# Two rows broadcast by way of DRAM, filler products on TensorE, and a later place for the sums in the first group of a graph-attention kernel

## The chip, the core and the metric

The kernel runs on one core of a Trainium2 chip. The core has five engines that run beside each other and wait for each other through semaphores: TensorE (PE, with its weight loads shown apart as PEld), VectorE (DVE), ScalarE (ACT), GpSimd (POOL) and SyncE (SP). Transfers between DRAM and the on-chip memory are issued from SP's and ScalarE's instruction streams and carried out by 16 DMA engines. The metric is the device time of one execution in microseconds (us); lower is better.

## What is computed

Two graph layers follow each other, on 64 graphs of 256 nodes with 512 features (x: 64 x 256 x 512, adj: 64 x 256 x 256, all float32). The first is a single-head attention in which the score of a pair of nodes is a sum of two numbers, q of the one and k of the other:

```python
feat_proj = einsum('bnh,oh->bno', feats, fc_w) + fc_b
q = einsum('bnh,oh->bno', feat_proj, q_w) + q_b
k = einsum('bnh,oh->bno', feat_proj, k_w) + k_b
masked = q + swapaxes(k, 2, 1) + (1.0 - adj) * -1e9
masked = where(masked >= 0, masked, 0.01 * masked)
x1 = einsum('bnm,bmh->bnh', softmax(masked), feat_proj) + feats
```

The second is an attention with 8 heads over x1, with the logarithm of the adjacency and a bias added to the scores, and x1 added to its output.

Since q and k are one number per node, the kernel does not go through feat_proj for them: it multiplies q_w and k_w with fc_w once, which gives two rows of 512 numbers, and takes the dot product of each node's features with these rows. The rows, here called q's row (`wq_row`) and k's row (`wk_row`), are needed in all 128 partitions. How they get there is what the change is about.

## The kernel before

The 64 graphs are worked in 32 groups of two (512 nodes, as T = 4 tiles of 128). A function `step` writes out by hand the order of all engines' work for one group's tail, the next group's middle and the one after it; inside the block `tc.manual_schedule` each engine takes its instructions in exactly the order of the program. Groups 1 to 31 take their first layer in pieces mixed with the heads of the group before. Group 0 has nothing to be mixed with, and its first layer is the function `features_first` (L678), which runs in the first 45 us or so. The changed lines all lie there or ahead of it.

**Loads.** ScalarE issues the four pieces of fc_w, `fc_nat` (L225). SP issues q_w, k_w and fc_b (L231), x of group 0 (L206), b_q and b_v (L231), q_b and k_b (L138), the four pieces of adj of group 0 (L201), then the weights wq, wk and wv of 1 MB each (L143) and `wgc_row` (L138). The adj pieces of group 1 (L201) follow in `step`. An adj piece is 128 KB in runs of 128 bytes.

**Warm-up and rows.** TensorE first multiplies the identity with itself six times (L1143, result unused), turns the small vectors into columns (`columns`, L249), and then `rows_of_x` (L257) forms both rows at once: four products accumulate in one PSUM bank, the product with piece `oc` of `fc_nat` as soon as that piece has landed (L261). ScalarE copies the 2 x 512 result to the on-chip memory (L266). `constant` (L279) forms a small constant `kqc`; its end, `k_constant`, is called later.

**Spreading.** `spread_rows` (L269) is called after the first tile of x has been transposed (L691). For each row, a product with a column of the identity, repeated 128 times, puts the row into all partitions of a PSUM bank (L273), and ScalarE copies it out (L277).

**features_first**, in the order of its engines:

- TensorE transposes the four tiles of x (`xTp`, L686; VectorE copies them, L687) and fc_w (`pfc`, L152; ScalarE copies it to `fcT`, L153). `product(t)` forms feat_proj of tile t (`fp`, L699; ScalarE copies it, L703).
- VectorE takes the dot products with q's row (`dot_q`, four instructions L519, in the trace `jq`), then `k_constant` (L291), then those with k's row (`dot_k`, `jk`), then `adjt` (the transposed adjacency L557 and the mask L559).
- `queries` (L572): four TensorE transposes spread q of the nodes along the free axis (L576), and ScalarE copies the result to `qrow` (L581).
- `weights(jc)` (L593), for two halves: VectorE adds q, k and mask (L599) and applies the slope (L603), ScalarE takes the Exp (L604). The result `e0` holds the unnormalised attention. `add_eps` (L570) prepares the adjacency for the second layer.
- `constants_of_projections` (L295): products of fc_b with wq and wv (`pc`, L301). Its end, `add_constants` (L310), transposes the result (`pct`, L313) and adds it to the bias columns (VectorE, L317 and L318).
- `blocks_of_weights` (L327): sums of blocks of wk, wq and later wv and fcT on VectorE (L335 to L338).
- `sums` (L633): products of a column of ones with `e0` (L639) give the softmax sums, ScalarE copies them (L644). `recip_of_sums` (L646): one transpose (`rc`, L648), and VectorE's reciprocal (L649).
- For each tile t, the product of `e0` with feat_proj (`x1p`, L731), two of the block sums on VectorE, the scaling and the addition of x (VectorE, L737), and then the transpose of the new x (`x1Tp`, L792) with ScalarE's copies (L797).

After this, `step` begins the second layer of group 0 with the first product of Q (`pq`, L412).

**Later groups** spread q of the nodes in another way, `spread` (L583): SP writes the 512 numbers to DRAM (`q`, L586) and reads them back to all partitions (`qrow`, L588).

PSUM is used in four single banks (`bank`) and two pairs. The constant's bank (`pk`) is kept from `constant` until `k_constant`.

Of the kernel before, what the change touches and what calls it, by code (L numbers as in the profile page):

```python
# [10 lines left out]
F32 = mybir.dt.float32  # L11
# [6 lines left out]
P = 128  # L18
# [7 lines left out]
def kernel(  # L26
# [64 lines left out]
    nc = tc.nc  # L91
    NB, N, D = x.shape
# [4 lines left out]
    NC = D // P  # L97
# [12 lines left out]
    const = ctx.enter_context(tc.tile_pool(name="const", bufs=1))  # L110
# [5 lines left out]
            name=nc.get_next_instruction_name(), act_func_set_id=both[0], ins=[], outs=[]  # L116
# [4 lines left out]
    ident = const.tile([P, P], F32, tag="ident", name="ident")  # L121
# [24 lines left out]
    def transposed_weights(w, pool, psum, copy):  # L146

        t = pool.tile([P, NC, D], F32, tag="fcT", name="fcT")
        for hc in range(NC):
            pt = psum.tile([P, 512], F32, tag="bank", name=f"pfc_{hc}")  # L150
            for oc in range(NC):
                nc.tensor.transpose(pt[:, ts(oc, P)], w[:, oc, ts(hc, P)], ident)  # L152
            copy(t[:, hc, :], pt)  # L153
        return t

    wk_row = const.tile([P, D], F32, tag="wk_row", name="wk_row")
    wq_row = const.tile([P, D], F32, tag="wq_row", name="wq_row")
    kqc = const.tile([P, 1], F32, tag="kqc", name="kqc")

    NR = 4  # L160
# [3 lines left out]
    def fast():  # L164
        main = ExitStack()
        with main:
# [12 lines left out]
            def bank(name):  # L179
                return ps.tile([P, 512], F32, tag="bank", name=name)  # L180

            def pair(name):
                return psc.tile([P, 2, 512], F32, tag="pair", name=name)

            dram = main.enter_context(
                tc.tile_pool(name="dram", bufs=2, space=bass.MemoryType.DRAM)
            )
# [30 lines left out]
            for q in range(P // B):  # L218
                for n in range(P // B):
                    rows = slice(q * B, (q + 1) * B)  # L220
# [24 lines left out]
            def columns(rows, cols, name):  # L245

                n = rows.shape[0]
                pt = bank(name)
                nc.tensor.transpose(pt[:, 0:n], rows, ident[0:n, 0:n])  # L249
                nc.vector.tensor_copy(cols, pt[:, 0:n])  # L250
# [6 lines left out]
            def rows_of_x():  # L257

                pr = bank("rows_qk")[0:2, :]
                for oc in range(NC):  # L260
                    nc.tensor.matmul(  # L261
                        pr, lhsT=cols_0[:, oc : oc + NC + 1 : NC], rhs=fc_nat[:, oc, :],
                        start=(oc == 0), stop=(oc == NC - 1),
                    )
                rows = one.tile([2, D], F32, tag="junk", name="rows_qk_sb")
                nc.scalar.copy(rows, pr)  # L266
                return rows

            def spread_rows(rows):  # L269

                for n, dst in enumerate((wq_row, wk_row)):
                    pt = bank(f"row_{n}")
                    nc.tensor.matmul(  # L273
                        pt, lhsT=ident[0:2, n : n + 1].to_broadcast([2, P]), rhs=rows,
                        start=True, stop=True,
                    )
                    nc.scalar.copy(dst, pt)  # L277

            def constant():  # L279

                both = two.tile([P, NC], F32, tag="c", name="qk_col")
                part = two.tile([P, 2, T], F32, tag="kq", name="qk_fcb")
                nc.vector.tensor_tensor(both, qw_col, kw_col, ALU.add)
                nc.vector.tensor_tensor(both, both, fcb_col, ALU.mult)
                nc.vector.tensor_reduce(part[:, 0, 0:1], both, AX.X, ALU.add)
                pk = bank("pk")
                nc.tensor.matmul(
                    pk[:, 0:1], lhsT=part[:, 0, 0:1].to_broadcast([P, P]), rhs=ones[:, 0, 0:1],
                    start=True, stop=True,
                )  # L290
                return lambda: nc.vector.scalar_tensor_tensor(  # L291
                    kqc, pk[:, 0:1], qb, kb, ALU.add, ALU.add
                )
# [232 lines left out]
            class Group:  # L526
# [151 lines left out]
                def features_first(self):  # L678

                    g = self.g  # L680
                    xT = one.tile([P, NC, TOK], F32, tag="qT", name=f"xT_{g}")
                    fp = v_all
                    for t in range(T):
                        pt = bank(f"xTp_{g}_{t}")
                        for c in range(NC):
                            nc.tensor.transpose(pt[:, ts(c, P)], self.x[:, t, ts(c, P)], ident)  # L686
                        nc.vector.tensor_copy(  # L687
                            xT[:, :, ts(t, P)], pt.rearrange("p (c n) -> p c n", c=NC)
                        )
                        if t == 0:  # L690
                            spread_rows(rows_qk)  # L691
                    fcT = transposed_weights(fc_nat, wts, ps, nc.scalar.copy)
                    for t in range(T):
                        self.dot_q(t)

                    def product(t):
                        pp = bank(f"fp_{g}_{t}")
                        for c in range(NC):
                            nc.tensor.matmul(  # L699
                                pp, lhsT=xT[:, c, ts(t, P)], rhs=fcT[:, c, :],  # L700
                                start=(c == 0), stop=(c == NC - 1),
                            )
                        nc.scalar.copy(fp[:, t, :], pp)  # L703

                    product(0)
                    self.queries()
                    k_constant()
                    for t in range(T):
                        self.dot_k(t)
                    self.adjt(True)  # L710
                    product(1)
                    self.weights(0)
                    self.weights(1)
                    self.add_eps()
                    product(2)
                    add_constants = constants_of_projections()
                    for name, wt in (("k", wk_sb), ("q", wq_sb)):
                        for issue in blocks_of_weights(wt, name):
                            issue()
                    self.sums()  # L720
                    columns(rows_1, cols_1, "cols_1")
                    product(3)
                    add_constants()
                    self.recip_of_sums()
                    self.begin()
                    sums = blocks_of_weights(wv_sb, "v") + blocks_of_weights(fcT, "fc")
                    for t in range(T):
                        gr, ic = divmod(t, TPG)
                        po = bank(f"x1p_{g}_{t}")
                        for j in range(TPG):  # L730
                            nc.tensor.matmul(  # L731
                                po, lhsT=self.e0[:, j, gr, ts(ic, P)], rhs=fp[:, gr * TPG + j, :],
                                start=(j == 0), stop=(j == TPG - 1),
                            )
                        for issue in sums[2 * t : 2 * t + 2]:
                            issue()
                        nc.vector.scalar_tensor_tensor(  # L737
                            self.x[:, t, :], po, recip0[:, g, t : t + 1], self.x[:, t, :],
                            ALU.mult, ALU.add,
                        )  # L740
                        if t > 0:
                            self.x1t(t - 1)
                    self.x1t(T - 1)
# [393 lines left out]
            with tc.manual_schedule(engines=ENGINES):  # L1137
                f = Group(0)
                f.x, f.a = x_0, adj_0

                warm = bank("warm")
                for n in range(6):
                    nc.tensor.matmul(warm[:, 0:P], lhsT=ident, rhs=ident, start=True, stop=True)  # L1143
                columns(rows_0, cols_0, "cols_0")
                rows_qk = rows_of_x()
                k_constant = constant()
                d, a, a_w = None, None, {}
                for g in range(NG):
                    n = Group(g + 1) if g + 1 < NG else None

                    def check():

                        if d is not None and (d.g % NR == NR - 1 or d.g == NG - NR // 2 - 1):
                            in_range(d.g // NR * NR, d.g + 1, f"{d.g}")

                    step(d, a, f, n, check)
                    d, a, f = a, f, n
# [215 lines left out]
```

## Time and profile before

| What | us |
|---|---|
| runs of the kernel | 2314.91, 2314.97, 2316.4 |
| median of the runs | 2314.97 |
| the profiled execution, own time | 2316.6 |
| its span, first to last instruction | 2314.8 |
| busy in the span: TensorE, VectorE, ScalarE, GpSimd | 2298.1, 2111.0, 1073.2, 122.5 |
| first `pq` product of group 0 on the chain of waits | 45.23 |

The profiled execution is one execution; its span leaves out what lies before the first and after the last instruction, 1.8 us. Its mean granted TensorE clock is 0.997 of full speed.

A row of the timeline or of the chain begins with the start in us from the start of the span and the duration in us; then come the engine, the line, the operation, the tile written and the tiles read. In brackets stands how long the engine was idle before it and what ended that. "PE row L273 x4" are the four instructions of the two row products: a float32 product is two instructions. In a table by stretches of time, each engine's busy time is followed by the number of its instructions; PEclk is the clock that TensorE was granted, and the DMA share is the mean busy share of the 16 DMA engines (a little over 1 where packets overlap). "SPq" and "ACTq" are the instruction streams of SP and ScalarE from which transfers are issued. In the view of the waits a line says who waited for whom: us in total, times, longest.

### The profile page before, as it was taken

How to read it: one execution, taken by the hardware profiler on the slowest of the kernel's cores; microseconds unless marked ns; L12 is line 12 of the kernel's file. 1: busy time of each engine (PE TensorE's matmuls, PEld its weight loads, DVE VectorE, ACT ScalarE, POOL GpSimd, SP SyncE). 2: the span in 40 equal slices, each digit the busy share in tenths (PEclk: the TensorE clock that was granted, in tenths of full speed). 3: DMA queues.
4: the chain of work that ended last, by engine and by line, in shares of the span. 5: the costliest groups of instructions: out<-in, count | busy, mean ns of one | idle time of the engine just before them, and what ended most of it. 6: DMA issues, size and time to landing. Idle time of an engine off the chain costs nothing.

```text
span 2314.8 us, 33829 instructions
## 1 busy us (share of the span) xinstructions
PE 2298.1 (99%) x12738; PEld 1910.7 (83%) x12738; DVE 2111.0 (91%) x3150; ACT 1073.2 (46%) x1865; POOL 122.5 (5%) x120
## 2 busy tenths in 40 slices
PE   9999999999999999999999999999999999999997
PEld 5888888888888888888888888888888888888885
DVE  6899999999899999999999999999999999999997
ACT  3544445444445444444444454444544444444443
POOL 0000000000000000000000000000000000000000
PEclk9999999999999999999999999999999999999999
DMA  4122323323323232232233232332323323323312
GB/s 132 42 64 73 78 73 69 65 65 84 80 63 70 60 78 78 73 66 63 69 78 82 60 74 63 79 78 74 64 60 73 78 74 69 69 61 84 81 46 38
DMA packets 517265, 163.85 MB, mean 71 GB/s; under 512 B 415188, under 2 KB 478696, under 8 KB 517096
## 3 DMA queue, kind: packets, MB, share of 16 engines
q1 hardware_dynamic: 514440, 160.32, 29.4%
q8 instruction: 103, 1.69, 0.3%
q10 hardware_dynamic: 2656, 1.31, 0.2%
q14 instruction: 66, 0.54, 0.1%
HBM read 95.43 MB, written 66.12 MB: 70 GB/s over the span
## 4 chain that ended last, share of the span: by engine, by line
PE 97%; DVE 1%; DMA 1%; ACT 0%; issue 0%; SPq 0%; ACTq 0%; DVEq 0%
PE pv L412 17%; PE pq L412 16%; PE pf L412 16%; PE pk L412 16%; PE sc L840 11%; PE oT L880 10%; PE y L670 9%; PE fp L699 1%; DMA fc_nat<-in_L_gnn_fc_w_dram 0%; PE tot L907 0%; PE rc L624 0%; DMA xd<-xt 0%; PE xTp L686 0%; DVE osb L1003 0%; DVE osb L1009 0%; DVE osb L1002 0%
## 5 line engine op out<-in xcount | busy, mean ns | idle before, releaser
L854 ACT ACTIVATE e<-sc,c 128x1024 f32<-128x1024 f32 x254 | 269.0, 1110 | 81.7 <-PE sc L840 80.2
L860 DVE TENSOR_TENSOR e<-e,am 128x1024 f32<-128x1024 f32 x254 | 297.8, 1213 | 0.4 <-ACT e L854 0.4
L840 PE MATMUL sc<-qT,kT 64*128 64x256 f32 x2048 | 255.8, 389 | 0.3 <-ACT e L854 0.3
L880 PE MATMUL oT<-e,v 128*64 128x256 f32 x2032 | 233.4, 382 | 0.0
L495 POOL TENSOR_TENSOR pf_s<-pf_s,x 128x512 f32<-128x512 f32 x93 | 119.0, 1279 | 2110.4 <-ACT pf_s L494 1980.7
L670 PE MATMUL y<-e,x 128*128 128x256 f32 x992 | 226.1, 382 | 0.0
L840 PEld LDWEIGHTS sc<-qT,kT 64*128 64x128 f32 x2048 | 187.2, 186 | 42.5 <-issue 21.2
L880 PEld LDWEIGHTS oT<-e,v 128*64 128x64 f32 x2032 | 140.2, 137 | 85.4 <-issue 18.6
L670 PEld LDWEIGHTS y<-e,x 128*128 128x128 f32 x992 | 186.1, 190 | 24.0
L432 ACT ACTIVATE pq_s<-pq,cols 128x256 f32<-128x256 f32 x192 | 80.6, 471 | 249.6 <-PE pq L412 249.6
L494 ACT ACTIVATE pf_s<-pf,recip 128x256 f32<-128x256 f32 x186 | 78.1, 471 | 197.4 <-PE pf L412 197.4
L897 DVE TENSOR_REDUCE part<-est 128x32 f32<-128x1024 f32 x124 | 151.3, 1220 | 4.3
L896 DVE STREAM_TRANSPOSE est<-es 128x1024 f32<-128x1024 f32 x124 | 152.3, 1229 | 0.0
L867 DVE TENSOR_TENSOR es<-e,e 128x1024 f32<-128x1024 f32 x126 | 149.3, 1205 | 1.1
L676 ACT COPY yT<-y 128x512 f32<-128x512 f32 x124 | 72.7, 587 | 131.4 <-PE y L670 130.6
L429 ACT COPY pk_s<-pk 128x512 f32<-128x512 f32 x96 | 56.3, 587 | 164.2 <-PE pk L412 164.2
L887 ACT COPY oTs<-oT 128x512 f32<-128x512 f32 x128 | 75.1, 587 | 117.0 <-PE oT L880 96.2
L443 DVE TENSOR_TENSOR qT<-pq,pq_s 128x512 f32<-128x512 f32 x96 | 66.2, 690 | 64.0 <-ACT pq_s L432 39.5
L412 PE MATMUL pk<-t1b,wk 128*128 128x256 f32 x512 | 121.1, 379 | 0.4 <-DVE kT L443 0.4
L412 PE MATMUL pq<-x1T,wq 128*128 128x256 f32 x512 | 121.0, 379 | 0.3 <-DMA x1T<-xd 0.3
L412 PE MATMUL pv<-wv,t1b_c 128*128 128x256 f32 x512 | 121.1, 379 | 0.0
L412 PE MATMUL pv<-wv,t1b 128*128 128x256 f32 x512 | 121.1, 379 | 0.0
(180 smaller groups left out, 4563.3 us busy)
## 6 DMA issues: line engine op xcount, KB each, us to landing
x<-in_x_dram SPq DMA_DIRECT2D x32, 1024.0 KB, 5.1
out_dram<-osb SPq DMA_DIRECT2D x254, 128.0 KB, 3.3
xd<-xt SPq DMA_DIRECT2D x124, 256.0 KB, 2.0
x1T<-xd SPq DMA_DIRECT2D x496, 64.0 KB, 1.9
adj<-in_adj_dram SPq DMA_DIRECT2D x128, 128.0 KB, 3.6
qrow<-q SPq DMA_DIRECT2D x31, 256.0 KB, 4.0
fc_nat<-in_L_gnn_fc_w_dram ACTq DMA_DIRECT2D x4, 256.0 KB, 5.0
wq<-in_L_gnn_W_q_dram SPq DMA_DIRECT2D x1, 1024.0 KB
```

Source lines behind the costliest of these rows:

```text
L412: nc.tensor.matmul(o, lhsT=lk[:, ts(m, P)] if len(lk.shape) == 2 else lk[:, m], rhs=rk, start=(start and m == 0 and k == 0), stop=(m == 1 ...
L432: nc.scalar.activation(dst[:, m], src[:, m], AF.Identity, bias=self.bias[:, 2 * o + m : 2 * o + m + 1],)
L494: nc.scalar.mul(s[:, m], src[:, m], self.recip[:, TPG * k + m : TPG * k + m + 1])
L495: nc.gpsimd.tensor_tensor(s, s, self.out(o, k), ALU.add)
L670: nc.tensor.matmul(y[:, ts(gr, N)], lhsT=self.x[:, gr * TPG + j, ts(c, P)], rhs=self.e0[:, j, gr, :], start=(gr == 0 and j == 0), stop=(gr ...
L840: nc.tensor.matmul(sc[:, par, pr, :], lhsT=self.kT[rows, 2 * hg + pr, ts(t, P)], rhs=self.qT[rows, 2 * hg + pr, ts(gr, N)], start=True, st ...
L854: nc.scalar.activation(e, sc, AF.Exp, bias=self.c[:, t : t + 1], scale=SCALE)
L860: nc.vector.tensor_tensor(ef, ef, self.am[:, jc, u // 2, :].unsqueeze(1).to_broadcast([P, 4, N]), ALU.mult,)
L867: nc.vector.tensor_tensor(self.esum[u], self.e[u, 0], self.e[u, 1], ALU.add)
L880: nc.tensor.matmul(oT[par * HD : (par + 1) * HD, pr, :], lhsT=self.v[:, gr * TPG + jc, ts(h, HD)], rhs=self.e[2 * gr + hg, jc][:, par, pr, :],
L896: nc.vector.transpose(turned, self.esum[u].rearrange("p a b i -> p (a b i)"))
L897: nc.vector.tensor_reduce(self.part[:, hg, :], turned.rearrange("p (m c) -> p m c", c=B), AX.X, ALU.add,)
```

## The change

- The two rows become two halves of one tile, `qk_rows`.
- `rows_of_x` issues two idle products (the identity with itself, as in the warm-up) after each of the first three row products. The warm-up itself becomes a call of the same function, `keep_going`.
- `spread_rows` has no products and no copies out of PSUM any more. ScalarE's stream issues a write of the two rows (4 KB) to a tile in DRAM and a read of that tile to all 128 partitions (4 KB each, 512 KB in all). It is called right after `rows_of_x`, ahead of the transposes of x, instead of after the first of them.
- `queries` moves from before `k_constant` and the products with k's row to after `product(1)`.
- `sums` moves from before `columns(rows_1, ...)` and `product(3)` to after them.
- `recip_of_sums` moves from before the loop over the tiles into it, after the first `x1p` products on TensorE and ahead of the first two block sums on VectorE.

```diff
-    wk_row = const.tile([P, D], F32, tag="wk_row", name="wk_row")
-    wq_row = const.tile([P, D], F32, tag="wq_row", name="wq_row")
+    qk_rows = const.tile([P, 2, D], F32, tag="qk_rows", name="qk_rows")
+    wq_row, wk_row = qk_rows[:, 0], qk_rows[:, 1]
...
                         start=(oc == 0), stop=(oc == NC - 1),
                     )
+                    if oc < NC - 1:
+                        keep_going(2)
...
             def spread_rows(rows):
 
-                for n, dst in enumerate((wq_row, wk_row)):
-                    pt = bank(f"row_{n}")
-                    nc.tensor.matmul(
-                        pt, lhsT=ident[0:2, n : n + 1].to_broadcast([2, P]), rhs=rows,
-                        start=True, stop=True,
-                    )
-                    nc.scalar.copy(dst, pt)
+                d = dram.tile([2 * D], F32, tag="qk", name="qk_rows_d")
+                nc.scalar.dma_start(d.rearrange("(n h) -> n h", n=2), rows)
+                nc.scalar.dma_start(
+                    qk_rows.rearrange("p n h -> p (n h)"), d.unsqueeze(0).to_broadcast([P, 2 * D])
+                )
...
-                        if t == 0:
-                            spread_rows(rows_qk)
                     fcT = transposed_weights(fc_nat, wts, ps, nc.scalar.copy)
...
                     product(0)
-                    self.queries()
                     k_constant()
                     for t in range(T):
                         self.dot_k(t)
                     self.adjt(True)
                     product(1)
+                    self.queries()
                     self.weights(0)
                     self.weights(1)
...
-                    self.sums()
                     columns(rows_1, cols_1, "cols_1")
                     product(3)
+                    self.sums()
                     add_constants()
-                    self.recip_of_sums()
                     self.begin()
...
+                        if t == 0:
+                            self.recip_of_sums()
                         for issue in sums[2 * t : 2 * t + 2]:
                             issue()
...
-                for n in range(6):
-                    nc.tensor.matmul(warm[:, 0:P], lhsT=ident, rhs=ident, start=True, stop=True)
+
+                def keep_going(count):
+                    for n in range(count):
+                        nc.tensor.matmul(warm[:, 0:P], lhsT=ident, rhs=ident, start=True, stop=True)
+
+                keep_going(6)
                 columns(rows_0, cols_0, "cols_0")
                 rows_qk = rows_of_x()
+                spread_rows(rows_qk)
                 k_constant = constant()
```

## The prediction

> **What bounds the kernel now.** I read the page first. TensorE is busy for 99% of the span, so only what moves the start of its steady work can count.
>
> ```profile
> PE 2298.1 (99%) x12738; PEld 1910.7 (83%) x12738; DVE 2111.0 (91%) x3150; ACT 1073.2 (46%) x1865; POOL 122.5 (5%) x120
> ```
>
> The change touches group 0 alone, which ends where the first pq product starts at 45.23 us. From there TensorE runs without a gap for 30 us, so a shift of that start is a shift of the end. The chain of waits over the first 90 us (start us, us, what) shows what sets it.
>
> ```profile
> 11.94 1.91 PE row L273 x4
> 13.85 2.24 PE xTp L686 x12
> 16.09 2.68 PE pfc L152 x16
> ...
> 35.59 0.23 PE pct L313 x2
> ...
> 35.85 0.37 DVE cols L317 x4
> ...
> 43.76 0.71 DVE x L737
> ...
> 45.23 1.73 PE pq L412 x8
> ```
>
> TensorE leads to 35.8 us, then VectorE for 8.6 us. The reader should next see how little room VectorE had before that. Its timeline:
>
> ```profile
> 16.13 0.69 DVE L687 COPY xT<-xTp 128x512 f32<-128x512 f32 x1 [0.16 <-PE xTp L686]
> 16.73 0.68 DVE L519 CUSTOM_DVE_ANT_0 jq<-x,wq_row 128x512 f32<-128x512 f32 x1
> ...
> 34.48 0.16 DVE L250 COPY cols<-cols 128x8 f32<-128x8 f32 x1
> 35.85 0.36 DVE L317 TENSOR_TENSOR cols<-cols,pct 128x2 f32<-128x2 f32 x4 [1.21 <-PE pct L313]
> ```
>
> From the first dot product with q's row (16.73) to 34.64 us VectorE works 17.07 of 17.91 us, in order and with no wait. Then it waits 1.21 us for TensorE, the only slack. So two chains end almost together: TensorE's with 0 slack, VectorE's with 1.21 us, and the second starts with the very rows that now go through DRAM.
>
> **What the change does to the rows.** Removed: two row products (four instructions, 1.91 us of TensorE's chain) and two ScalarE copies of 0.59 us. Added on ScalarE's queue: a 4 KB write to DRAM and, after it has landed, a read of 512 KB to 128 partitions. When can the write start? The rows are in SBUF at 11.60 us now (copy at 11.03, 0.57 us). But issues here also wait for older transfers:
>
> ```profile
> SPq L201 <- DMA x<-in_x_dram: 5.1, 1, 5.1
> SPq L231 <- DMA rows<-in_L_gnn_k_w_dram: 0.7, 1, 0.7
> SPq L231 <- DMA rows<-in_L_gnn_q_w_dram: 0.6, 1, 0.6
> ...
> SPq L138 <- DMA rows<-in_L_gnn_fc_b_dram: 0.3, 1, 0.3
> ```
>
> Nothing in adj_0 needs x, yet its first issue waited 5.1 us for x. Counting SP's and ScalarE's issues in one order (q_w, k_w, fc_b, fc_nat, x, three fc_nat, b_q, b_v, q_b, k_b, four adj, wq, wk, wv, wgc_row), all four rows fit one rule: an issue waits for the landing of the eighth before it. By that rule the write, after wgc_row, waits for the first adj piece, the read for the second. In the DMA views (KB each, us to landing):
>
> ```profile
> adj<-in_adj_dram SPq DMA_DIRECT2D x1, 128.0 KB, 3.2
> q<-kq SPq DMA_DIRECT2D x31, 2.0 KB, 1.4
> qrow<-q SPq DMA_DIRECT2D x31, 256.0 KB, 4.0
> ```
>
> The first line is adj's issue at 11.19 us: it lands at 14.4. The other two are the same detour as later groups make it. Write: 1.4 us is the nearest row, and up to 2.0 (the 256 KB xd writes) with adj on the engines; I take 1.6, so it lands at 16.0. Read: 256 KB took 4.0 us in a quiet stretch (3.2 to 4.3), bytes moving for about 2.3 us of that. The engines are not quiet here (length, busy us of PE, PEld, DVE, ACT, POOL, then clock, DMA share, GB/s):
>
> ```profile
> 15.00:16.00 1.00, 1.00 (x7) 1.00 (x6) 0.86 (x2) 0.00 (x0) 0.00 (x0) 0.50 1.10 170
> 20.00:21.00 1.00, 1.00 (x4) 0.46 (x3) 0.96 (x3) 0.00 (x0) 0.00 (x0) 1.00 1.04 403
> ```
>
> The weights fill all 16 engines. If the two queues share equally, half of 403 GB/s moves 524 KB in 2.6 us; with the 1.7 us (4.0 less 2.3) that do not scale that is 4.3. Twice the quiet transfer gives 1.7 + 4.6 = 6.3. And 256 KB of fc_nat took up to 7.8 us on ScalarE's queue beside x. Bounds: 4.0 and 7.8; I take 5.4, between the first two as nearest in kind. The rows land at 14.4 + 1.6 + 5.4 = 21.4 us.
>
> [...]
>
> **VectorE's sum.** The same instructions in the same order now start at 21.4 instead of 16.73: 4.7 us later. The 1.21 us wait goes, if TensorE is done by then: **+3.5 us**.
>
> **Is TensorE done by then?** Queued behind the read's issue on ScalarE are the four fcT copies. ScalarE is free at about 16.4 (write landed 16.0, issue 0.3 to 0.4), and the copies started at 16.98, so they come at most 0.6 us earlier, although TensorE is ready sooner. fp 0, which needs them, gains as little: it ends near 21.7 instead of 22.2. Then fp 1 (3.44) to 25.1; the transposes of q moved behind it need dot products done at 21.4 + 2.8 = 24.2, so they cost only their 0.44. fp 2 to 29.0, pc 1.86, columns 0.15, fp 3 3.63: 34.7. The sums come here and need the second Exp: now at 29.60, with VectorE 4.7 later 34.3, so 0.44 and no wait; in their old place, near 31, they would have held fp 3 for 3 us. The pct transposes end at about 35.4, x1p 0 (1.8) at 37.2, the moved rc transpose at 37.4. VectorE reaches L317 at 34.64 + 4.7 = 39.3. Done by then, with 2 us to spare after rc. The weights, landed before 29 now, come 1.3 us later (524 KB at 403 GB/s); pc needs them at 29.0, so up to 1 us of that spare is used.
>
> **Idle products.** Six, of two instructions each as in the warm-up (12 instructions for 6): 12 x 0.244 (2.93/12, early) = 2.9 us, or 12 x 0.15 (x1Tp, 0.60/4) = 1.8 us later. TensorE idles only 0.86 us between the row products, so the rows come 0.2 to 1.0 us later than 11.60. Cost 0: the write waits until 14.4 anyway; without that wait the full delay. Their aim shows in the first window row above: granted clock 0.50 (0.68 before it, 0.61 at 17 us). Full clock would bring xTp and pfc from 2.24 + 2.68 to the 28 x 0.15 = 4.2 us of x1Tp: 0.7 us of TensorE, which VectorE's chain hides here.
>
> [...]
>
> Lateness has a price of its own: TensorE then idles some 3 us waiting for the first x. The cut clock after 14.3 us lasted 3.4 us, so between 0 and 1.7 us; I take 0, since that chain is paced by VectorE, whose steps (2.0 us an x tile) leave TensorE's 0.6 + 1.8 almost covered. One tile in place of two holds the same rows, and SP's later loads now look eight back past two more transfers, all long landed by then (adj_1's at 24 us or later wait for adj_0, wq and wk): 0.
>
> **Sum.** Against the profiled execution: span 2314.8, 1.8 around it, 2316.6 in all; with +3.5 the span is 2318.3. The median of the runs, 2314.97, lies 1.6 below that execution and moves alike: **2318.5**.
>
> **Rivals.**
> *No wait for older transfers* (the count restarts or the order differs). Rows in SBUF at 12.1 with idle products, write to 13.6, read at 5.2, a little under 5.4 since the weights have hardly begun: 18.8. VectorE +2.1, less 1.21: +0.9, 2315.9. Against it stand the four rows above.
> *The read starves* behind 3 MB of queued weights. It takes the 7.8 us of the worst fc_nat piece: landing 23.8, VectorE +7.1 - 1.2 = +5.9, with the clock's 1.7 up to +7.6: 2320.9 to 2322.6, slower. It decides once the rows land after 22.6 (+4.66). For it: DMA share 1.04 to 1.07 from 19 to 25 us; against it: a queue of its own, which from 4 to 8 us gave fc_nat 28 to 32% of the engines beside x's 47 to 57%.
> *The rows are in time* and TensorE's freed 1.91 us show. They must land by 16.7, so within 4.6 us of leaving the copy at 12.1, under the 1.4 + 4.0 of the quiet detour. Even then the reciprocal, now behind x1p 0 (1.8 us) on TensorE, comes no sooner than now, and the x chain follows it: only the clock's 0.7 us remain, 2314.3.
> *It does not do what it says*: the clock falls to half anyway. Same time as the forecast.
>
> **How the numbers follow.** Forecast (landing 20.0 to 22.6, +2.1 to +4.6): 0.45. No old wait: 0.19. Starved: 0.32. In time: 0.04. The likeliest gives 2318.5, its own range 2317.0 to 2319.6. The range for 8 in 10 runs to the other cases, 2315.3 to 2321.8: below it lie the cases in time and some early ones, above it the starved with a slow clock. A measurement tells from no change about 0.2%, 4.6 us. Starved is beyond that, with a little of the forecast: slower 0.34. Faster by 4.6 us has no source: 0.02. Within: 0.64.
>
> **What would show it.** The first jq on VectorE near 21 us with its wait put down to the rows' transfer; ScalarE's write issued at about 14.4 after 2 us or more of nothing; fcT's first copy near 16.5; the 1.21 us before L317 gone; pq's start near 48.7. Wrong would be a first jq before 19 (no old wait, or a quick read), a wait at L317 or L649 that names TensorE, or any change between groups after the first pq.

## The result and the profile after

| | before | after |
|---|---|---|
| median of the runs, us | 2314.94 (2313.94 to 2317.22, 9 runs) | 2320.65 (2318.37 to 2324.87, 9 runs) |
| ratio after to before, 95% interval | | 1.0025 [1.0016, 1.0033] |
| the profiled execution: own time, span | 2316.6, 2314.8 | 2319.11, 2317.3 |

The change makes the kernel slower by 5.7 us at the median, 0.25%. The two profiled executions differ by only 2.5 us: the one of before is 1.7 us above its median, the one of after is 1.5 us below its own. The nine times of after stand apart: four from 2318.4 to 2319.1, one at 2320.65, four from 2322.2 to 2324.9. So there are two questions: where the 2.5 us of the profiled pair come from, and why many executions of after lose 3 to 6 us more.

The page's busy row of after shows that the work is the same: TensorE's busy time is 0.4 us more (12 instructions for the idle products, 4 fewer for the row products), GpSimd's 0.4 us more, VectorE's and ScalarE's 1.6 and 1.7 us less.

```profile
PE 2298.5 (99%) x12746; PEld 1910.1 (82%) x12746; DVE 2109.4 (91%) x3150; ACT 1071.5 (46%) x1863; POOL 122.9 (5%) x120
```

From the first pq on almost nothing changes: in the fourteen profiled executions of this study the span less the start of that instruction on the chain of waits is 2269.0 to 2269.9 us (2269.6 before, 2269.3 after). So everything below is about group 0. Next, ScalarE's timeline of after (start us, us, engine, line, operation, tiles, and in brackets the idle time before and what ended it).

```profile
11.17 0.58 ACT L268 COPY rows_qk_sb<-rows_qk 2x512 f32<-2x512 f32 x1 [9.14 <-PE rows_qk L261]
11.78 0.51 ACTq L274 DMA_DIRECT2D qk_rows_d<-rows_qk_sb  x1
13.48 0.36 ACTq L275 DMA_DIRECT2D qk_rows<-qk_rows_d  x1
14.02 2.27 ACT L153 COPY fcT<-pfc 128x512 f32<-128x512 f32 x4 [2.27 <-PE pfc L152]
```

The write is issued 0.03 us after the copy of the rows: it waits for no older transfer. The read, which waits for the write to land (the chains of three kernels below show it behind the write's 4.77, 2.36 and 2.79 us), follows 1.70 us after the write's issue. VectorE's timeline of after shows what the rows and the moved reciprocal do:

```profile
18.94 0.69 DVE L519 CUSTOM_DVE_ANT_0 jq<-x,qk_rows 128x512 f32<-128x512 f32 x1 [4.48 <-issue]
...
36.60 0.16 DVE L250 COPY cols<-cols 128x8 f32<-128x8 f32 x1
37.26 0.36 DVE L317 TENSOR_TENSOR cols<-cols,pct 128x2 f32<-128x2 f32 x4 [0.50 <-PE pct L313]
...
39.09 0.18 DVE L649 RECIPROCAL recip<-rc 128x4 f32<-128x4 f32 x1 [1.27 <-PE rc L648]
```

The first jq starts 2.21 us later than before (16.73). The idle time ahead of it is put down to "issue", yet ScalarE and TensorE had long done what it needs: it is the read, which the traces of three kernels below name at this place. L250 is 2.12 us later (34.48 before). The wait at L317 shrinks from 1.21 to 0.50 us, and a new one of 1.27 us appears at the reciprocal. 2.12 - 0.71 + 1.27, and 0.09 for the order of the small instructions, make the reciprocal's 2.77 us (39.09 against 36.32), and pq is 2.74 us later. The chain of waits of after:

```profile
15.42 13.52 DMA wv<-in_L_gnn_W_v_dram
28.93 0.04 issue
28.98 2.97 PE pc L301 x28
31.95 0.20 PE cols L249
32.15 4.12 PE fp L697 x8
36.27 0.57 PE sm L639 x16
36.85 0.37 PE pct L313 x2
37.22 1.72 PE x1p L728 x4
38.94 0.12 PE rc L648
39.06 0.02 issue
39.09 0.18 DVE recip L649
...
47.97 1.73 PE pq L412 x8
```

TensorE, ahead of VectorE's chain in the forecast, ends last after all. pc waits for wv, and then pc takes 2.97 us instead of 1.86, with the granted clock at 0.50 from 29.7 us on. The tables by stretches of after (length, busy us of PE, PEld, DVE, ACT, POOL, granted clock, DMA share, GB/s) show the cut, and that it is gone from where the kernel before had it:

```profile
15.00:16.00 1.00, 1.00 (x8) 0.76 (x7) 0.00 (x0) 0.99 (x3) 0.00 (x0) 1.00 1.17 266
...
30.00:31.00 1.00, 1.00 (x14) 0.52 (x8) 0.96 (x3) 0.00 (x0) 0.00 (x0) 0.50 0.82 129
```

The clock at 15 us was 0.50 before and is 1.00 now. That the idle products keep it there is not shown. In the timelines of the five profiled kernels without them, pfc takes 2.88 us in before, with the cut, and 3.05 in the one with the reciprocal alone moved, but 2.29 with the DRAM spreading alone and 2.42 with the queries alone, against 2.29 in after; in the one without idle products below, its last 14 instructions take 2.01 us, against 2.02 with the DRAM spreading alone. From 29.7 to 33.1 us a half clock (0.50) falls on pc and fp 3. SP's queue of after has the issue of wv:

```profile
14.87 0.51 SPq L143 DMA_DIRECT2D wk<-in_L_gnn_W_k_dram  x1
15.42 2.98 SPq L143 DMA_DIRECT2D wv<-in_L_gnn_W_v_dram  x1
```

The issue of wv took 0.51 us before and takes 2.98 us now, ending at 18.40, half a microsecond before the rows are there. In that stretch the engines still move the short pieces of adj: from 16 to 19 us, 1056 of 1265 packets are under 512 bytes, while in the kernel before there are none between 17 and 19 us. So the read runs beside adj as well as beside the weights. That the long issue made wv late is not shown: with the gap filled (below) the same issue took 1.03 us, and TensorE got wv later still, at 29.49. The read's 512 KB on the same engines, and adj of group 1, issued at 26.34 with wv not yet in, are other candidates.

### The profile page after: what moved, and what is told of

It is laid out like the page before. It is cut to its first block, busy times and chain, and to the rows that moved or that the text cites. A ratio compares the mean times of both kernels' runs of the same rounds, so it can differ in the third digit from the quotient of the medians.

```text
span 2317.3 us, 33846 instructions
## 1 busy us (share of the span) xinstructions
PE 2298.5 (99%) x12746; PEld 1910.1 (82%) x12746; DVE 2109.4 (91%) x3150; ACT 1071.5 (46%) x1863; POOL 122.9 (5%) x120
## 4 chain that ended last, share of the span: by engine, by line
PE 97%; DVE 1%; DMA 1%; SPq 0%; ACT 0%; issue 0%; DVEq 0%
PE pv L412 17%; PE pq L412 17%; PE pf L412 16%; PE pk L412 16%; PE sc L839 11%; PE oT L879 10%; PE y L670 9%; DMA wv<-in_L_gnn_W_v_dram 1%; DMA x<-in_x_dram 0%; PE tot L906 0%; PE fp L697 0%; PE rc L624 0%; PE pc L301 0%; SPq L201 0%; DVE osb L1002 0%; DVE osb L1008 0%
## 5 line engine op out<-in xcount | busy, mean ns | idle before, releaser
L839 PEld LDWEIGHTS sc<-qT,kT 64*128 64x128 f32 x2048 | 187.2, 186 | 42.5 <-issue 21.2
```

Of the source, the lines that this page charges most:

```text
L839: nc.tensor.matmul(sc[:, par, pr, :], lhsT=self.kT[rows, 2 * hg + pr, ts(t, P)], rhs=self.qT[rows, 2 * hg + pr, ts(gr, N)], start=True, st ...
```

## The experiments

Four theories stood at first: the rows come late; the weights come late to pc; the clock falls at another place; the moves of queries and reciprocal, or the idle products, cost by themselves. In the texts of the first four runs V is the first of these, W the second and third together, and M the fourth; later letters are explained where they stand. The runs of before beside the experiments have medians of 2315.25 (first four), 2314.69 (next four), 2314.87 (next three) and 2315.11 (last).

**The whole change but the spreading.**

```diff
-    spread_rows by DRAM, right behind rows_of_x
+    spread_rows by two products, behind xTp of tile 0
```

> The rows are spread by the two products again; the idle products, the later queries, sums and reciprocal stay as in the change. Theory W (the 512 KB read pushes the weights back, TensorE reaches pc before wv has landed, stands idle for 2 us, and the clock is cut behind that): no wait at pc, first jq at 16.7 us or a little sooner, pq starts at 44 to 45.5 us, 2313.5 to 2315.5 us, runs as close together as those of the kernel before (3 us). Rival V (VectorE's late start alone costs): the same, 2314 to 2315. Rival M (the moved sums and reciprocal or the idle products cost): still 2318 or more.

Measured: 2318.25 (2317.48 to 2320.92), ratio 1.0017 [1.0008, 1.0026]. So 3.0 us are lost without any DRAM detour, as only M had it: the moves and the idle products have a cost of their own. VectorE's timeline of this kernel names both moves:

```profile
26.30 1.26 DVE L601 SCALAR_TENSOR_TENSOR e<-qrow,kq,e 128x256 f32<-128x256 f32 x2 [1.68 <-ACT qrow L583]
...
38.13 0.18 DVE L651 RECIPROCAL recip<-rc 128x4 f32<-128x4 f32 x1 [1.53 <-PE rc L650]
```

1.68 us of waiting are due to the queries behind fp 1, 1.53 us to the reciprocal behind x1p 0. The second is easy to follow on TensorE: x1p 0 starts at 36.00, released by VectorE's own copy of the columns (L250, at 35.78), and the reciprocal's transpose comes behind it, at 37.82. So VectorE stands still for about as long as x1p 0 takes.

**The DRAM spreading alone, in the kernel before.**

```diff
-    two products and two ScalarE copies behind xTp of tile 0
+    write and read on ScalarE's queue, right behind rows_of_x
```

> The kernel before with only the spreading through DRAM; no idle products, nothing moved. W: queries stand ahead of fp 1 and wait for the late dot products (21.9 us), so TensorE comes to pc only near 29 us, when wv has landed; no idle there, but a stop of some 2 us ahead of queries, after which the clock may fall. First jq near 19, pq near 46 to 48, 2316 to 2318.5. V: first jq 2.2 us late less the 1.2 us of slack, 2316. M: as before, at most 2316.

Measured: 2316.39 (2315.45 to 2317.79), ratio 1.0006 [0.9997, 1.0015]: at most 0.15% slower. The first jq starts at 17.86, 1.1 us later than before, and 0.73 us of that are taken from VectorE's slack (the wait at the bias columns is 0.48 us instead of 1.21).

**Idle products into the gap before pc**, and **pc behind fp 3**. Both start from the changed kernel and go for TensorE's wait for wv:

```diff
                    product(2)
+                   fill = bank("fill")
+                   (8 products of the identity with itself)
                    add_constants = constants_of_projections()
```

> The change with eight more idle products (about 2.4 us) between fp 2 and pc, where TensorE waited for wv. W with the clock as the main price: pc begins at 29.0 as in the change but runs at full clock, pc 1.9 us instead of 3.0, fp 3 3.5 instead of 4.1, granted clock 1.00 from 29 to 35 us; 1.5 to 3.5 us faster than the change (2317 to 2319) and the runs within 3 us of each other instead of 6.5. If the wait alone is the price, or V: no faster than the change, 2320 to 2321. M: the same as the change or a little slower.

```diff
                    product(2)
+                   product(3)
                    add_constants = constants_of_projections()
...
-                   product(3)
                    self.sums()
```

> The change with fp 3 ahead of pc, so TensorE has 3.5 us of work while wv lands. W: no idle TensorE at 27 to 29 us, no cut clock, rc done near 34.5 us, so VectorE's chain is the bound again: pq near 46.3, 2315.5 to 2317, runs within 3 us. V: the same time as the change, 2320 to 2321, since the first jq stays at 19. M: the same as the change.

Measured: the first 2320.99 (2317.99 to 2325.73), ratio 1.0026 [1.0016, 1.0036]; the second 2318.57 (2316.97 to 2322.34), 1.0017 [1.0008, 1.0026]. Neither comes down to what W forecast. With the gap filled pc's later pairs of instructions take 0.39 us in the timeline, as in before, and not up to 0.65 as in after, but a half clock falls on x1p 0 instead (granted 0.50 from 38.6 to 42.0 us; 3.23 us instead of 1.72), and the chain of waits is no shorter (pq at 50.3). With pc late, TensorE falls out of the chain; VectorE's timeline of that kernel has no wait from the first jq on:

```profile
19.90 0.69 DVE L519 CUSTOM_DVE_ANT_0 jq<-x,qk_rows 128x512 f32<-128x512 f32 x1 [4.93 <-issue]
...
37.60 0.16 DVE L250 COPY cols<-cols 128x8 f32<-128x8 f32 x1
37.86 0.36 DVE L317 TENSOR_TENSOR cols<-cols,pct 128x2 f32<-128x2 f32 x4
38.26 0.16 DVE L318 TENSOR_TENSOR cols<-cols,cols 128x4 f32<-128x4 f32 x1
38.33 0.18 DVE L649 RECIPROCAL recip<-rc 128x4 f32<-128x4 f32 x1
```

From here the arithmetic is simple: the reciprocal starts 18.4 us after the first jq where nothing waits (19.90 and 38.33 here, 18.75 and 37.14, 21.30 and 39.71 in two kernels below), and pq 8.9 us after that. In these kernels it is the landing of the rows that sets the end.

**One move at a time.** First the changed kernel with the reciprocal back in its old place, then each of three parts alone in the kernel before:

```diff
-                   (changed kernel) recip_of_sums behind x1p 0
+                   recip_of_sums between add_constants and begin
```

> The change with the reciprocal's transpose back ahead of the first x1p product. Theory R (x1p 0 waits for a PSUM bank or for TensorE's queue, and the reciprocal waits behind it while VectorE stands still: 1.3 us in the change's trace, 3 us when the clock is cut there): VectorE's wait ahead of the reciprocal gone, pq 1.2 us earlier for the same first jq, median 1.3 to 3 us under the change: 2317.5 to 2319.5. Rival V (only the landing of the rows counts): as the change, 2320 to 2321. Rival W (only the wait for wv counts): as the change.

```diff
-                   (kernel before) recip_of_sums ahead of begin
+                   recip_of_sums behind x1p 0
```

> The kernel before with nothing but the reciprocal moved behind the first x1p product. R: VectorE stands still 1.2 us (rc after 1.8 us of x1p instead of before it) ahead of the reciprocal, first jq unchanged at 16.7, 2316.2 to 2316.8. V and W: no change, 2315.2.

```diff
                    (kernel before) rows_of_x
+                   if oc < NC - 1: keep_going(2)
```

> The kernel before with nothing but the six idle products between the row products. If they keep the clock: granted clock 1.00 from 14 to 18 us, xTp and pfc 0.7 us shorter, first jq 0.3 to 0.6 us earlier and TensorE 0.7 us earlier at pct: 0.3 to 0.7 us faster, 2314.5 to 2314.9. If the clock falls after the transposes anyway: the row result up to 0.4 us later and the same time or up to 0.5 slower, 2315.2 to 2315.7.

```diff
                    (kernel before) product(0)
-                   self.queries()
...
                    product(1)
+                   self.queries()
```

> The kernel before with nothing but the transposes of q moved behind the second feat_proj product. With the rows in time VectorE would wait for qrow ahead of the first weights: qrow at about 27.2 instead of 23.8, VectorE there at 25.0, 2.2 us of wait less the 1.2 of slack: 1.0 slower, 2316.2. If TensorE is the bound at that point, no change: 2315.2.

| | median (range) | ratio, 95% interval |
|---|---|---|
| reciprocal back in the changed kernel | 2320.11 (2317.14 to 2324.57) | 1.0024 [1.0015, 1.0033] |
| reciprocal alone | 2317.05 (2315.34 to 2318.87) | 1.0008 [0.9999, 1.0017] |
| idle products alone | 2316.09 (2313.96 to 2317.81) | 1.0004 [0.9995, 1.0013] |
| queries alone | 2316.65 (2315.51 to 2319.72) | 1.0008 [0.9998, 1.0017] |

No part alone can be told from no change with certainty; their medians add 2.4, 1.4 and 2.0 us, and the DRAM spreading 1.1 us. Taking the reciprocal back gains little at the median, 0.5 us, against what was expected of that theory. But its profiled execution has its rows at the same time as that of after (18.98 and 18.94) and is 1.6 us quicker (2317.51 against 2319.11), and its quickest run is 1.2 us quicker than after's. So, by this one pair of executions, the move costs about 1.5 us where the rows come early; the median must be set by something else. And the times still lie in two bunches, 2317.1 to 2318.9 and 2320 to 2324.6.

That spread is the clue. The kernels with both the DRAM spreading and the idle products have it (ranges of 5.4 to 7.7 us: the changed kernel, the two with pc's gap changed, the reciprocal back). Those with one of the two alone keep within 2.3 to 3.9 us. It is a weak clue: the runs of before, 9 to 33 at a time, range over 2.9 to 5.7 us themselves. The last four runs are about this.

**The read ahead of the weights, the weights ahead of the read, and no idle products.** All three start from the kernel with pc late, so that VectorE's chain alone sets the end.

```diff
             adj_0 = load_adj(0)
-            wq, wk, wv, wgc_row loads
...
-                nc.scalar.dma_start(
+                nc.sync.dma_start(
                     qk_rows.rearrange("p n h -> p (n h)"), ...
...
                 spread_rows(rows_qk)
+                wq, wk, wv, wgc_row loads
```

> Base: the changed kernel with pc and its columns behind fp 3 (e4_pc_late), whose runs spread over 5.4 us (2317.0 to 2322.3). Here the read of the rows is issued on SP, between adj_0 and the weights, so that no weight can be ahead of it. Theory W (the spread and the lateness come from how much of the 3 MB of weights is queued when the read starts): read issued near 14.3, behind adj's four pieces alone, rows land at 17.5 to 18.8, recip 36.0 to 37.2, median 2316.2 to 2317.5, spread of the runs under 3.5 us. Rival C (it comes from where the 3.41 us windows of half clock fall, and the landing is steady): median at most 1 us below e4_pc_late, spread still 5 us. Rival D (the read is slow whatever it meets): rows at 19.5 or later, 2318 or more.

```diff
+            wq, wk, wv, wgc_row loads
             adj_0 = load_adj(0)
-            wq, wk, wv, wgc_row loads
```

> Base e4_pc_late; wq, wk, wv and w_g's row are issued ahead of adj_0, near 11 us, so that all of the weights are ahead of the read on every execution. Theory W: the read (issued near 13.5) lands at 21 to 24, recip at 38.33 + (landing - 19.9), median 2319.6 to 2322.6, that is, at the upper bunch of e4_pc_late's runs. Rival C: landing 19 to 20.5, median within 1 us of e4_pc_late (2317.6 to 2319.6), two bunches as before. In both cases adj lands late, up to 23 us, and may hold the adjt step; a wait of VectorE or TensorE that names adj is then to be taken off.

```diff
-                    if oc < NC - 1:
-                        keep_going(2)
```

> Base e4_pc_late, without the six idle products. Theory W: the rows leave TensorE 0.6 us earlier, the read gets ahead of one weight more; landing 17.9 to 19.3, median 2316.5 to 2318, fewer runs above 2321. Rival C: the clock is cut to half near 14 us as in the kernel before, xTp and pfc take 0.7 us longer, which VectorE's chain hides: the same median as e4_pc_late within 0.5 us, the same spread.

| | median (range) | ratio, 95% interval |
|---|---|---|
| read first | 2318.68 (2317.12 to 2319.68) | 1.0014 [1.0005, 1.0023] |
| weights first | 2321.56 (2321.13 to 2325.03) | 1.0030 [1.0019, 1.0042] |
| no idle products | 2316.67 (2315.57 to 2322.51) | 1.0010 [1.0001, 1.0019] |

With the weights first, the median is at the upper bunch, as expected, and no run is below 2321. The chain of waits of that kernel:

```profile
11.27 0.58 ACT rows_qk_sb L268
11.85 0.02 issue
11.87 4.77 DMA qk_rows_d<-rows_qk_sb
...
16.72 6.85 DMA qk_rows<-qk_rows_d
...
23.70 0.69 DVE jq L519
```

4 KB take 4.77 us to land, and the read 6.85 us; the first jq is at 23.70, 3.8 us later than with pc late alone. (Further on, this chain runs over a transfer of adj and over x1p 0 at half clock, 3.11 us with 0.50 granted from 39 to 40 and from 41 to 42 us, but both together make the reciprocal wait only 0.57 us: 23.70 + 18.4 + 0.6 is its 42.7.) With the read first the spread falls from 5.4 to 2.6 us, as expected, but the median, which was to be 2316.2 to 2317.5, hardly moves, and the rows land at 21.2 in the profiled execution instead of 17.5 to 18.8. Those are the numbers given for theory D (a read that is slow whatever it meets), yet the read took only 4.69 us. The chain of waits of that kernel shows what else is late:

```profile
4.89 1.87 PE rows_qk L257 x2
6.75 1.15 PE warm L1140 x4
7.91 1.80 PE rows_qk L257 x2
9.71 1.16 PE warm L1140 x4
10.86 0.95 PE rows_qk L257 x2
11.81 0.64 PE warm L1140 x4
12.46 0.96 PE rows_qk L257 x2
13.44 0.58 ACT rows_qk_sb L264
14.05 2.36 DMA qk_rows_d<-rows_qk_sb
16.48 4.69 DMA qk_rows<-qk_rows_d
```

In this execution the first products on TensorE take twice their later time (1.87 against 0.95 us, 1.16 against 0.64) until 10.8 us. In the profiled execution of after only the first pair is slow, 1.45 us, and all takes the shorter time from about 6 us. This is called a slow start below. What causes it is not shown: the times are about doubled, as those of x1p 0 are at a granted 0.50 (3.78 us in the kernel with twice the idle products, 1.88 in the timeline of after at 1.00), but the table by stretches gives 1.00 there, as it does in the first 12 us of before and of after:

```profile
7.00:8.00 1.00, 1.00 (x5) 0.70 (x5) 0.00 (x0) 0.00 (x0) 0.00 (x0) 1.00 1.03 376
```

The write is slow here too, 2.36 us, with adj under way (its last issue ended at 13.98) and no weight issued yet (wq at 16.86): a late write meets adj as well. The rows leave TensorE at 11.2 us in one execution and at 13.4 us in another, and two of the four slow stretches are idle products. Without idle products there is room for a slow start. In the kernel with the DRAM spreading alone the first two row products (four instructions) took 2.90 us, in the one without idle products 1.91; yet the next product waited for `fc_nat` in both (0.69 and 1.87 us), and ScalarE's copy began at 11.04 in the first, as early as the kernel before. The kernel without idle products gains 1.9 us over the one with them (1.5 us when each is set against the runs of before beside it; the intervals overlap), and 9 of its 11 times lie within 1.9 us. The two others are at 2319.12 and 2322.51, so a long time occurs without idle products too.

**Twice the idle products**, in the changed kernel itself: the rows late in every execution.

```diff
-                        keep_going(2)
+                        keep_going(4)
```

> The changed kernel with twelve idle products between the row products in place of six: three times 0.64 us more at full clock, so the rows leave ScalarE's copy near 13.1 to 13.7 instead of 11.75, when wq and wk are on the engines. Theory W (late rows meet the weights, as the late rows of a slow clock do): the 4 KB write takes 3 us or more to land instead of 1.7 (in e10_weights_first 4.8), the read 6 to 7 us instead of 5.4, landing 22.5 to 25.5 with full clock early on, median 2322 to 2325.5, the lower bunch (2318.4 to 2319.1 of the changed kernel) gone. Rival P (a plain delay): write 1.7 and read 5.5, landing 20.6 to 21.2, median 2322 to 2323 but both bunches there, shifted by 1.9: lowest runs at 2320.3. The row that tells them apart is the time from the write's issue to the read's issue on ScalarE's queue, and the first jq.

Measured: 2325.97 (2324.76 to 2328.72, 5 runs), ratio 1.0050 [1.0036, 1.0064]; 0.5 us above the top of what the collision was to give, and the lower bunch is gone. The chain of waits:

```profile
12.65 0.58 ACT rows_qk_sb L268
13.23 0.02 issue
13.25 2.79 DMA qk_rows_d<-rows_qk_sb
...
16.06 7.61 DMA qk_rows<-qk_rows_d
...
41.85 3.78 PE x1p L728 x4
45.63 0.23 PE rc L648
45.88 0.18 DVE recip L649
```

The rows leave ScalarE 1.5 us later than in after, the first jq (23.92) starts 5.0 us later: write and read take 10.4 us together instead of 7.1. A plain delay would have been 1.5. (The write stayed just under the 3 us expected, the read went above 6 to 7.) So 5.0 of the 6.8 us by which pq is later are the rows. The rest is x1p 0 with the half clock on it (granted 0.50 from 41 to 46 us): TensorE waited 2.5 us for the columns ahead of x1p 0, x1p 0 took 3.78 us instead of 1.72, and the reciprocal, behind it, waited 3.43 us.

What stays open: no profiled execution of the changed kernel is one of its upper bunch. That these are the executions with a slow start, whose rows then meet the weights, is argued from the three kernels above; it was not seen in a trace of the changed kernel itself. A rival is a half clock that falls on x1p 0, with the reciprocal behind it. The profiled execution with the gap filled, at 2321.39, lies above the lower times of its kernel (2318.0 to 2319.0), and its rows left TensorE early:

```profile
10.98 0.57 ACT L268 COPY rows_qk_sb<-rows_qk 2x512 f32<-2x512 f32 x1 [8.95 <-PE rows_qk L261]
...
37.97 3.23 PE x1p L731 x4
```

Its first jq is at 20.03, 1.1 us later than in after, and most of the rest of its 2.4 us (pq at 50.34) is the wait behind the slow x1p 0, 2.88 us against the 1.77 that VectorE waits for TensorE in after. So a time above the lower bunch needs no slow start, and how often each of the two occurs is not known. Of a version quicker than before there is no sign: every kernel tried has its median 1.1 us or more above it.

## Why the prediction came out as it did

The forecast was 2318.5 with a range of 2315.3 to 2321.8. The time, 2320.65, lies in it, 2.2 us above the value. It lies in neither case's own range, though: it is above the forecast's (to 2319.6) and just below the starved read's (from 2320.9). The direction and the carrier were right (slower, by way of VectorE's dot products waiting for the rows), but two steps of the sum failed, and in the profiled execution they partly cancel: the rows came 2.5 us sooner than the sum had them, and VectorE waited 1.77 us (0.50 and 1.27) for TensorE, which the sum put at nothing. What is left is +2.5 us there against +3.5. That the median lands in the stated range is in part luck, then.

- **"The write waits for the first adj piece" failed.** It was to be issued at 14.4 and was issued at 11.78. The four rows of before fitted a count over SP's and ScalarE's issues; where the new write stands in that count was an assumption, and the idle time of 0.03 us ahead of it shows nothing was waited for. That was the rival without old waits, with rows at 18.8; they came by 18.94.
- **The write and the read** were 1.6 and 5.4 us; measured 1.70 and 5.4 (13.48 to about 18.9). The two sizes were right for a read that starts beside adj and before most of the weights. Issued ahead of the weights and 2.5 us behind the end of adj's last issue (the read first), the read took 4.69 us; with all weights issued ahead, 6.85 and 7.61. The forecast's upper bound of 7.8 and the rival "the read starves" were thus real in the two kernels that put all weights ahead of the read.
- **"TensorE is done by then, 2 us to spare" failed.** The reciprocal's transpose was to end at 37.4 and ended at 39.06, and VectorE waited for it. Up to pc the sum was right in its total, by luck: pc was put at 29.0 and began at 28.98, but it came there another way. TensorE was through fp 2 at 26.3, since the fcT copies began at 14.02 and not at 16.4; it did the first products with wq and then stood still for 2.07 us until wv had landed. The term that was mis-sized is the price of lateness, taken as 0 of 0 to 1.7: a half clock (0.50 from 29.7 to 33.1 us) came behind that pause, and pc and fp 3 took 2.97 + 4.12 us instead of 1.86 + 3.63, 1.6 us more.
- **"Costs only their 0.44" for the queries** held in after, whose Exp waits for the rows anyway, and was wrong with the rows in time (1.68 us of waiting). The same with the reciprocal: 1.5 us at early rows, nothing at late ones where pc is late (the timeline above).
- **"Idle products cost 0"** rested on the wait for adj; the text's alternative, the full delay, is what happened. Against the 0.2 to 1.0 us given, the copy of the rows began 0.14 us later than before in the profiled execution of after, 0.65 us later with pc late, and 2.41 us later with the read first, where the idle products behind the first two of the row products took their slow time (1.15 and 1.16 us against 0.64). The clock stayed at 1.00 from 14 to 18 us, worth nothing behind VectorE's chain, as said; 32 instructions of transposes in a row, from 11.31 to 15.45 us, ran at 1.00. In the kernel before, the clock fell at 14.36 us, 0.6 us into a stretch of transposes that stands behind 1.9 us of row products.
- **"The median moves alike" failed.** Profile to profile the loss is 2.5 us, median to median 5.7. The profiled execution of before is one with a half clock on xTp and pfc, and it has 1.21 us of slack at L317; the kernel with the idle products alone, whose rows are still spread by products and whose xTp and pfc behind them take 1.53 and 2.42 us instead of 2.31 and 2.88, has 0.50 us there. If the median execution of before is like that one, it has 0.7 us less of this slack to give; no run shows it.
- **The rivals were taken as alternatives, and one kernel may have both.** The rows land early in the profiled execution, as in the case without old waits, but not with the +0.9 us that went with it, since the moves were costed at nothing; and the times from 2322.2 up are where the starved read was put (2320.9 to 2322.6) and beyond, though no trace shows that they have one. That one kernel would spread over 6.5 us was not foreseen.

## What to carry to other kernels

The detour through DRAM at the start of this kernel was as long as what happened to be queued ahead of it made it (write and read 7.1 us in after, 11.6 with the weights first): ask not only how long the transfer takes, but which loads its issue is racing with, and what makes its source late. Filler work put ahead of such an issue was not free even on an engine that waited (the rows' copy came 0.14 to 2.41 us later), and at the start of the kernel it took up to twice its later time (1.16 us against 0.64). Before adding a profile's difference to the median of the runs, check that the slack the sum uses is in the typical execution and not only in the profiled one.

## What was not expected of the hardware

- A 4 KB write to DRAM took 1.70 us to land beside adj, 2.36 us beside adj when issued 2.3 us later (the read first), 2.79 us beside adj with wq, wk and wv issued behind it (at 13.93, 14.67 and 15.22 us, the write at 13.25), and 4.77 us beside the 3 MB of weights (wq and wk issued ahead of it, wv right behind).
- An issue on SP took longer while the other queue's read of 512 KB to 128 partitions was under way: 2.98 us instead of 0.51 for wv; 3.35 us for wq in the kernel without idle products. In after, adj's short packets were on the engines in the same stretch (1056 of 1265 packets from 16 to 19 us), and which of the two holds the issue is not shown; with the read first, on SP's own queue and 2.5 us behind the end of adj's last issue, the longest issue behind it took 1.29 us.
- Behind pauses of TensorE of 2.49 and 1.66 us (weights first), 1.83 (gap filled) and 2.07 (after) stood a half clock of 3.4 us, which began 0.5 to 0.7 us behind the end of the pause; all but the one behind 2.49 fell on work that VectorE waited for. With twice the idle products it began near 40.2 us, inside a pause of 2.52 us that ended at 41.85, and was still there at 46. The length of the pause does not decide it: behind 1.97 us (pc late) x1p 0 took its usual 1.88 us in the timeline, and behind 2.24 us (reciprocal back) the first two x1p took 3.60, as in before.
